# Later near sums and chunk ends in the second pass over the adjacency matrix, and the constants of the ranking as a scheduled step

## The chip, the cores and the metric

The kernel runs on one core of a Trainium2 chip. The metric is the device time of one execution in microseconds (us). The core has five engines with queues of their own that run beside each other and wait for each other by semaphores: TensorE (PE, matrix products), VectorE (DVE), ScalarE (ACT), GpSimd (POOL, here mostly the issuer of gathers) and SyncE (SP, the issuer of the large loads). Transfers run on 16 DMA engines.

## The reference

Four layers of a graph network follow each other on the same graph with N = 2708 nodes and 128 features. Each ends with a layer normalization of `x + layer(x)`. Cut to what matters here, the first two are:

```python
# layer 0
z  = leaky_relu(lap_mul(A, x) @ W1 + b1, 0.1)
S  = exp(-dist(z, z) / 2);  keep the 4 largest of each row, the rest 0
A2 = S + A
x  = layernorm(x + lap_mul(A2, x) @ W2 + b2)     # lap_mul(A, x) = d * (A @ (d * x)), d = rowsum(A) ** -0.5
# layer 1
XW = x @ W;  s_col = XW @ a[:128];  s_row = XW @ a[128:]
den = exp(leaky_relu(s_row[:, None] + s_col[None, :], 0.01))
num = A @ den
x  = layernorm(x + A @ ((den / num) @ XW))
```

All of it is in 32-bit floats. Layers 2 and 3 are products with the same `A`.

## The kernel before, in words

The 2708 rows are 22 tiles of 128 (the last has 20 rows); the columns are six chunks of 512, 512, 512, 512, 384 and 276, so that chunks 0 to 3 hold four tiles each and chunks 4 and 5 three each. The matrix is read as `adjT`. Six tiles of it stay in SBUF (`res`); the others come through a ring of four slots, filled by SP's loads (`load_panel`, L171 to L182).

The program has these stages: a first pass over the matrix (to about 165 us); the search for the four nearest nodes of each row (to about 300 us), where PE makes the distances, ACT copies them out and DVE finds the largest eight and their places (MAX8 and FIND_INDEX8, L649 and L650); the second pass, which multiplies by `A` again with the rows `y2` (295 to about 446 us); a ranking of the nodes, with a third pass (to about 530 us); and the second layer by blocks and the last layers.

The second pass is the place of the change. `by_panels` (L189) runs 132 products on PE: for each chunk, 16 tiles from the ring and five from `res`, and for the last tile's 20 rows three products at a time. A product of 512 columns is two passes on PE. After each product it calls `due.tick`. `Due` (L31 to L50) is a list of steps with a due number: `at(n, f)` puts step f at product n, and `tick` runs all steps that have come due, in the order of their numbers and, for equal numbers, of their entry. PE, DVE and ACT have a written order in this part (`manual_schedule`, L965): their instructions run in the order in which the steps issue them. An instruction of such a step can still stand between earlier instructions of the search, where the scheduler places it. POOL and SP have no written order.

The steps of a chunk c are these.

- `sum_near(t)` (L683), once for each tile t, at product `near_at[t]` (L915). It multiplies a row tile by the node's own weight (L686, DVE), has POOL gather three rows for each node from `y2_rows` in DRAM (`gather_near`, L675, issued at L677) and adds them with their weights (L690, DVE). The gathered rows have nine buffers.
- `end_pass2(c, acc)` (L922) is called when a chunk's products are done. It sets the product n at which the chunk ends: at least three products behind the near sum of its last tile, 16 behind the end of the chunk before, and not before the products are done.
- At n, `finish` (L927): `add_near` (L692, PE at L697) adds the near sums to the chunk's sum, and ACT copies it out to `hT` (L929).
- At n + 2, `norm0` (L734): PE multiplies by `w2` (L737), DVE adds and normalizes (L742, then L272 to L277; ACT takes a square root at L242).
- At n + 9, `turn` (L751, PE at L755, ACT's copy at L758); at n + 11, `find_c` (L806, PE at L809, ACT's copy at L810, DVE at L814).
- From n + 13, `compare` (L836, DVE), `times_w` (L819, PE at L822), `rank_rows` (ACT at L859) and `rank_columns` (PE at L864), some products apart for each tile, and `keep_xw` (L825), which stores rows to `xw_rows` from POOL's queue.

With the numbers before, the near sums stand at products 24, 28, 33, 37, 42, ... 120, and the chunks end at products 40, 59, 77, 96, 112 and 132.

Ahead of these steps, the constants of the ranking (L718 to L729) are written by DVE: a memset of `rk_f`, three additions for `fold`, and a memset and a copy for `sel`. They lie in the memory of `near`, which the search has written and which POOL still reads (L575 to L584, `others`) when it orders the neighbours.

Of the kernel before, what the change touches and what calls it, by code (L numbers as in the profile page):

```python
# [22 lines left out]
CH = 4  # L23
MAGIC = 1.5 * 2**23
OOB = 4095
# [5 lines left out]
class Due:  # L31
# [5 lines left out]
    def at(self, n, f, *args):  # L37
        self.work.append((n, len(self.work), f, args))
        self.work.sort(key=lambda w: w[:2])
# [13 lines left out]
def kernel(  # L53
# [16 lines left out]
    nc = tc.nc  # L70
    N, D = x.shape
    assert D == P
    T = (N + P - 1) // P
# [10 lines left out]
    NCH = NB // CH  # L84
# [51 lines left out]
    ident = const.tile([P, P], F32, tag="ident", name="ident")  # L136
# [227 lines left out]
    with tc.tile_pool(name="knn", bufs=1) as knn:  # L364
# [261 lines left out]
        with tc.tile_pool(name="keys", bufs=3) as keys:  # L626

            for n, t in enumerate([*range(4, S), *range(4), *range(S, T)]):
                p = pw[t]
# [89 lines left out]
    spare = near.rearrange("p t k -> p (t k)")  # L719
    few_n, rk_f, neg_r = (spare[:, n * T : (n + 1) * T] for n in range(3))  # L720
    fold, sel = spare[:, 3 * T : 3 * T + 2 * NCH], spare[:, 3 * T + 2 * NCH : 3 * T + 2 * NCH + 2 * NB]
    nc.vector.memset(rk_f, float(OOB))
    nc.vector.tensor_add(fold, ident[:, : 2 * NCH], ident[:, 32 : 32 + 2 * NCH])
    for g in (64, 96):
        nc.vector.tensor_add(fold, fold, ident[:, g : g + 2 * NCH])
    nc.vector.memset(sel, 0.0)
    nc.vector.tensor_copy(
        sel.rearrange("p (a v) -> p a v", v=2 * CH)[:, :, :2], fold.rearrange("p (a v) -> p a v", v=2)
    )  # L729
    nc.vector.memset(rows_d, 0.0)  # L730
    add_bias(b2_sb)
    rk = rk_pool.tile([P, T], F32, tag="rk", name="rk")
# [179 lines left out]

    due = Due()
    at = due.at
    near_at = [24 + (23 * t) // 5 for t in range(T)]  # L915
    for t in range(T):
        at(near_at[t], sum_near, t)

    ended = [-16]
    behind_last = []  # L920
# [794 lines left out]
```

## Time and profile before

| what | value |
| --- | --- |
| median of 6 runs | 1098.14 us (1093.43 to 1105.49) |
| profiled execution | 1095.9 us, span 1094.2 us |
| PE | 1003.5 us busy, 92% of the span |
| DVE | 641.3 us, 59% |
| ACT | 338.4 us, 31% |
| POOL | 262.8 us, 24% |
| granted clock of TensorE, mean | 0.969 |
| `add_near` of chunk 0 starts | 328.02 us |
| the last `add_near` starts | 444.63 us |

How to read it: times inside the profile are microseconds from the span's start. A line of the order of time gives the start, the duration, the engine, the line of the kernel, the operation, the tiles (out<-in) and their shapes, how many instructions were merged, and in brackets the idle time of that engine just before and what ended it. "issue" is a wait for which the profile shows no releaser; "remote" is one that ended with a signal whose sender the profile does not name. The ends of PE's products are modelled by the profile. The granted clock is 1 at full speed.

### The profile page before, as it was taken

To read this page: it belongs to the slowest core of one execution; us is meant where nothing else is said; L and a number is where in the kernel's file an instruction comes from. 1 tells how busy PE (TensorE), PEld (TensorE's weight loads), DVE (VectorE), ACT (ScalarE), POOL (GpSimd) and SP (SyncE) were. 2 spreads that over 40 slices of the span, in tenths; PEclk is the share of its full clock that TensorE was granted. 3 is DMA by queue.
4 is the path that set the end of the run, shared out by engine and by line. 5 is a ranking of instruction groups with operands and counts; after the bars stand their busy time and mean duration, and the time that the engine had idled before them with its cause. 6 is when DMAs were issued, how large, how long until landed. Compare 5 with 4: busy or idle time off the path is not lost.

```text
span 1094.2 us, 11460 instructions
## 1 busy us (share of the span) xinstructions
PE 1003.5 (92%) x3691; PEld 484.6 (44%) x3691; DVE 641.3 (59%) x1354; ACT 338.4 (31%) x617; POOL 262.8 (24%) x334
## 2 busy tenths in 40 slices
PE   0798999999997898798799999999999999999996
PEld 0345544444443455643233333334444644565444
DVE  5984448999943477773398999998112112132122
ACT  0000125555501144612466776665001100011000
POOL 4000000000465564006584444430112100000000
PEclk9989999999998999699899999999999999999998
DMA  9999330000184556497545545555675875574752
GB/s 341 362 323 281 108 124 1 0 1 1 49 277 133 162 179 190 151 343 257 134 130 160 147 126 161 143 153 181 220 241 150 278 224 187 171 234 160 240 160 75
DMA packets 109380, 190.31 MB, mean 174 GB/s; under 512 B 13666, under 2 KB 46706, under 8 KB 109310
## 3 DMA queue, kind: packets, MB, share of 16 engines
q1 hardware_dynamic: 91408, 151.79, 42.8%
q0 software_dynamic: 17728, 37.62, 12.4%
q8 instruction: 31, 0.51, 0.2%
q14 instruction: 39, 0.32, 0.1%
q10 hardware_dynamic: 174, 0.08, 0.0%
HBM read 214.37 MB, written 4.16 MB: 200 GB/s over the span
## 4 chain that ended last, share of the span: by engine, by line
PE 78%; DVE 7%; DMA 5%; issue 4%; ACT 2%; another core or an unknown queue 2%; POOL 1%; SPq 1%; POOLq 0%; DVEq 0%; ACTq 0%
PE acc L204 32%; PE num L1519 9%; PE hacc L1376 9%; PE acc L647 8%; PE acc L428 7%; DMA res<-in_adjT 3%; PE acc L637 2%; PE acc L1270 2%; PE mis L285 1%; DVE where L650 1%; DMA got<-y_rows,where 1%; DMA part<-in_adjT 1%; DVE near L649 1%; DVE both L483 1%
## 5 line engine op out<-in xcount | busy, mean ns | idle before, releaser
L1397 POOL DMA_INDIRECT ring<-in_adjT,slot_i x88 | 96.3, 1094 | 115.5 <-PE num L1519 87.2
L1519 PE MATMUL num<-ring,lw 128*64 128x512 f32 (+1 forms) x528 | 115.7, 560 | 3.0 <-DVE err L1361 1.6
L1376 PE MATMUL hacc<-inv,xws 128*128 128x512 f32 (+1 forms) x264 | 111.7, 559 | 0.6 <-issue 0.3
L647 PE MATMUL acc<-zT,z 128*128 128x512 f32 (+4 forms) x264 | 108.6, 558 | 0.0
L1351 ACT ACTIVATE inv<-num,plain 128x1024 f32<-128x1024 f32 x88 | 80.6, 915 | 60.9 <-PE num L1519 36.6
L253 POOL TENSOR_TENSOR rstd<-rstd,minus_half 128x4 f32<-128x4 f32 (+1 forms) x18 | 17.3, 960 | 313.4 <-DVE rstd L252 313.4
L648 ACT COPY key<-acc 128x512 f32<-128x512 f32 (+3 forms) x132 | 70.3, 535 | 59.8 <-issue 29.8
L234 ACT COPY gb<-acc 128x512 f32<-128x512 f32 (+2 forms) x18 | 9.6, 535 | 251.1 <-PE acc L204 251.1
L1361 DVE TENSOR_TENSOR err<-inv,num 128x1024 f32<-128x1024 f32 x88 | 74.4, 854 | 20.1 <-ACT inv L1354 17.7
L204 PE MATMUL acc<-ring,y 128*128 128x512 f32 (+2 forms) x192 | 81.3, 554 | 0.5 <-POOL sim L584 0.5
L1376 PEld LDWEIGHTS hacc<-inv,xws 128*128 128x128 f32 x264 | 46.5, 189 | 77.6 <-issue 47.9
L677 POOL DMA_INDIRECT got<-y_rows,where x66 | 69.7, 1057 | 39.7 <-DVE near_sum L690 16.9
L204 PE MATMUL acc<-ring,xs 128*128 128x512 f32 (+2 forms) x192 | 77.7, 548 | 0.0
L1368 DVE SCALAR_TENSOR_TENSOR inv<-gb,g_inv,inv 128x1024 f32<-128x1024 f32 x88 | 77.1, 914 | 0.1
L204 PE MATMUL acc<-ring,carry 128*128 128x512 f32 (+2 forms) x192 | 74.5, 542 | 0.0
L204 PE MATMUL acc<-ring,m_rows 128*128 128x512 f32 (+2 forms) x192 | 74.3, 542 | 0.0
L1365 DVE SCALAR_TENSOR_TENSOR inv<-err,inv 128x1024 f32<-128x1024 f32 x88 | 72.5, 862 | 0.1
L647 PEld LDWEIGHTS acc<-zT,z 128*128 128x128 f32 (+1 forms) x264 | 47.5, 188 | 54.9 <-issue 49.4
L1354 ACT ACTIVATE inv<-inv 128x1024 f32<-128x1024 f32 x88 | 67.6, 768 | 2.8
L649 DVE MAX8 near<-key 128x8 f32<-128x2708 f32 (+1 forms) x22 | 65.5, 2979 | 3.9 <-ACT key L648 3.9
L575 POOL TENSOR_TENSOR slot_e<-near,sim 128x44 f32<-128x44 f32 (+2 forms) x3 | 0.7, 244 | 273.9 <-DVE d2inv L603 267.2
L650 DVE FIND_INDEX8 where<-near,key 128x8 uint32<-128x2708 f32 (+1 forms) x22 | 65.4, 2973 | 0.0
(357 smaller groups left out, 1354.4 us busy)
## 6 DMA issues: line engine op xcount, KB each, us to landing
ring<-in_adjT SPq DMA_DIRECT2D x86, 1024.0 KB
ring<-in_adjT SPq DMA_DIRECT2D x19, 768.0 KB
part<-in_adjT SPq DMA_DIRECT2D x12, 1024.0 KB
ring<-in_adjT SPq DMA_DIRECT2D x19, 552.0 KB
res<-in_adjT SPq DMA_DIRECT2D x4, 1280.0 KB
more<-in_adjT SPq DMA_DIRECT2D x4, 1024.0 KB
part<-in_adjT SPq DMA_DIRECT2D x3, 768.0 KB
part<-in_adjT SPq DMA_DIRECT2D x3, 552.0 KB
```

What stands on the lines that cost most here:

```text
L204: nc.tensor.matmul(accs[c][: lhsT.shape[-1], :w], lhsT=lhsT, rhs=src, start=start, stop=stop)
L428: nc.tensor.matmul(accs[c][:, : cw[c]], lhsT=y[:, i, :], rhs=src[:, : cw[c]], start=first, stop=last)
L647: nc.tensor.matmul(pks[c][:p, : cw[c]], lhsT=z2[:, :p], rhs=zT[:, cs], start=False, stop=True)
L649: nc.vector.max(near[:p, t, :], key[:p])
L650: nc.vector.max_index(where[:p, t, :], near[:p, t, :], key[:p])
L1351: nc.scalar.activation(inv, num[:, :w], AF.Ln, scale=plain[:, 0:1], bias=plain[:, 1:2])
L1361: nc.vector.tensor_mul(err, inv, num[:, :w])
L1365: nc.vector.scalar_tensor_tensor(inv, err, 2.0, inv, op0=ALU.subtract, op1=ALU.mult)
L1368: nc.vector.scalar_tensor_tensor(inv, gb[:, col : col + w], g_inv[:, q : q + 1], inv, op0=ALU.max, op1=ALU.mult)
L1376: nc.tensor.matmul(haccs[:, o:e], lhsT=xws[:, q, :], rhs=inv[:, o:e], start=(q == 0), stop=(q == NQ - 1))
L1397: nc.gpsimd.indirect_dma_start(out=rows[i][:KC, n, :], out_offset=None, in_=adj_half[:, :], in_offset=bass.IndirectOffsetOnAxis(ap=slot_i[ ...
L1519: nc.tensor.matmul(num[n * (BJ + 2) : (n + 1) * (BJ + 2), o:e], lhsT=lw[:, 2 * q + n, :], rhs=rows[i][:, n, c0 + o : c0 + e], start=True, ...
```

## The change

Two things change. The near sums stand at products `31 + (17 * t) // 4`, that is 31, 35, 39, 43, 48, ... 120, a step of 4.25 products instead of 4.6; with the rules of `end_pass2` the chunks then end at products 46, 63, 80, 97, 113 and 132. And the six instructions for the ranking's constants become a function that is a step at product 27 (`near_at[0] - 4`).

```diff
@@ -719,14 +719,17 @@
     spare = near.rearrange("p t k -> p (t k)")
     few_n, rk_f, neg_r = (spare[:, n * T : (n + 1) * T] for n in range(3))
     fold, sel = spare[:, 3 * T : 3 * T + 2 * NCH], spare[:, 3 * T + 2 * NCH : 3 * T + 2 * NCH + 2 * NB]
-    nc.vector.memset(rk_f, float(OOB))
-    nc.vector.tensor_add(fold, ident[:, : 2 * NCH], ident[:, 32 : 32 + 2 * NCH])
-    for g in (64, 96):
-        nc.vector.tensor_add(fold, fold, ident[:, g : g + 2 * NCH])
-    nc.vector.memset(sel, 0.0)
-    nc.vector.tensor_copy(
-        sel.rearrange("p (a v) -> p a v", v=2 * CH)[:, :, :2], fold.rearrange("p (a v) -> p a v", v=2)
-    )
+
+    def set_constants():
+        nc.vector.memset(rk_f, float(OOB))
+        nc.vector.tensor_add(fold, ident[:, : 2 * NCH], ident[:, 32 : 32 + 2 * NCH])
+        for g in (64, 96):
+            nc.vector.tensor_add(fold, fold, ident[:, g : g + 2 * NCH])
+        nc.vector.memset(sel, 0.0)
+        nc.vector.tensor_copy(
+            sel.rearrange("p (a v) -> p a v", v=2 * CH)[:, :, :2], fold.rearrange("p (a v) -> p a v", v=2)
+        )
+
     nc.vector.memset(rows_d, 0.0)
@@ -912,9 +915,10 @@
     due = Due()
     at = due.at
-    near_at = [24 + (23 * t) // 5 for t in range(T)]
+    near_at = [31 + (17 * t) // 4 for t in range(T)]
     for t in range(T):
         at(near_at[t], sum_near, t)
+    at(near_at[0] - 4, set_constants)
```

## The prediction

> **What bounds the kernel now.** I read the chain of waits first: PE carries 78% of the chain that ended last, so a change pays only where it takes idle time or slow clock from PE. Then the waits of PE within the second pass (294 to 470 us), the largest of them:
>
> ```profile
> PE mis L737 <- issue: 5.4, 2, 4.7
> PE acc L697 <- issue: 4.4, 1, 4.4
> PE mis L755 <- DVE xs L277: 3.0, 1, 3.0
> PE mis L809 <- ACT xT L758: 2.6, 1, 2.6
> ```
>
> The columns are total us, times, longest. L697 is `add_near`, L737 `norm0`, L755 `turn`. All waits of PE up to the last `add_near` (444.63) come to 17.9 us; that is all the change can touch. Then the same stretch in order of time on each engine (start, us, engine, line, ..., idle time before it):
>
> ```profile
> 328.02 0.83 PE L697 MATMUL acc<-ident,near_sum 128*128 128x128 f32 x6
> 333.24 0.79 PE L697 MATMUL acc<-ident,near_sum 128*128 128x128 f32 x2 [4.38 <-issue]
> 333.82 3.62 PE L204 MATMUL acc<-res,y 128*128 128x512 f32 x4
> 338.20 2.08 PE L737 MATMUL mis<-w,hT 128*128 128x128 f32 x8 [0.76 <-issue]
> ...
> 343.97 3.60 PE L204 MATMUL acc<-ring,y 128*128 128x512 f32 x8
> 350.60 1.10 PE L755 MATMUL mis<-ident,xs 128*128 128x128 f32 x4 [3.04 <-DVE xs L277]
> ...
> 361.65 1.05 PE L697 MATMUL acc<-ident,near_sum 128*128 128x128 f32 x8
> ...
> 369.34 1.47 PE L737 MATMUL mis<-w,hT 128*128 128x128 f32 x8 [4.69 <-issue]
> ```
>
> ```profile
> 289.10 0.16 DVE L723 TENSOR_TENSOR near<-ident 128x22 f32<-128x22 f32 x1 [2.44 <-issue]
> ...
> 332.44 0.74 DVE L690 SCALAR_TENSOR_TENSOR near_sum<-got,sim,near_sum 128x128 f32<-128x128 f32 x2 [1.75 <-DMA got<-y_rows,where]
> ...
> 346.78 1.13 DVE L742 SCALAR_TENSOR_TENSOR xs<-mis,d2inv,xs 128x128 f32<-128x128 f32 x4 [9.51 <-remote]
> ```
>
> ```profile
> 337.56 0.59 ACT L929 COPY hT<-acc 128x512 f32<-128x512 f32 x1 [29.86 <-issue]
> ...
> 368.70 0.59 ACT L929 COPY hT<-acc 128x512 f32<-128x512 f32 x1 [6.12 <-remote]
> ```
>
> ```profile
> 342.86 1.00 POOL L677 DMA_INDIRECT got<-y_rows,where  x1 [0.30 <-issue]
> 352.17 1.00 POOL L677 DMA_INDIRECT got<-y_rows,where  x1 [8.31 <-DVE near_sum L690]
> ...
> 366.66 1.00 POOL L677 DMA_INDIRECT got<-y_rows,where  x1 [0.30 <-issue]
> ```
>
> Three things stand here. PE reaches the near sum of tile 3 at 328.85, but DVE has it at 333.18 (332.44 + 0.74). After that wait PE is slow: four passes of 512 columns take 3.62 us, 0.85 each, against 0.43 elsewhere; the window 320 to 340 shows a granted clock of 0.81. And three times PE's work reaches ACT or DVE late: `add_near` of chunk 0 ends at 334.03 and ACT copies at 337.56 (3.5 late); `norm0` ends at 340.28 and DVE starts at 346.78 (6.5 late); `add_near` of chunk 1 ends at 362.70 and ACT copies at 368.70 (6.0 late). Each waits for PE alone in the built program. Two of them end 1.0 and 2.9 us after POOL's unbroken runs of gathers (last ends 343.86 and 367.66). I do not know the cause; that the late ones go with these runs is an inference.
>
> **The change part by part.**
>
> Constants (six vector instructions). The edit says that they leave the search. The built order of the changed kernel says otherwise: the memset and the first addition still stand between the MAX8 of 283.70 and the FIND_INDEX8 after it, the two other additions and the last pair where they were. Their wait of 2.44 us (by its place for POOL, which ends its last read of `near` at 289.04) is on the chain and stays. Cost 0; bounds -2.4 (it does leave) and +0.2 (the last pair on a later gap). Only one 0.27 us multiply of near sum 0 moves, from 304.47, a gap in which DVE waits for ACT until 305.44, to after the constants, where DVE waits 6.67 us for its first gathered row: 0.
>
> Near sums 0 to 4. In the built order DVE runs them in one row before `norm0` of chunk 0, as now, and POOL's gathers before them keep their order. Gathers, not due times, pace them, so near sum 3 is still done at 333.18: 0, bounds 0 and +1.
>
> End of chunk 0, product 40 to 46. PE now runs six more products, five from `res` and one from `ring`, before `add_near`. 12 passes at 0.43 are 5.16 us, so it arrives at 328.02 + 5.16 = 333.18, just as the sum is ready. The 4.38 us wait is filled with work, and the slow passes after it go too. But nothing behind it comes sooner: `add_near` at 333.2, ACT's copy at 337.56, `norm0` at 338.20, DVE at 346.78, the first normalized tile at 350.56, `turn` at 350.60. PE reaches `norm0` at 334.1 + 1.7 = 335.8 and waits 2.4, then does `norm0` (1.05) and seven products (6.02), is at `turn` at 345.3 and waits 5.3 where it waited 3.04. At 350.60 it is six products further: -5.16.
>
> End of chunk 1, product 59 to 63. `norm0` of chunk 1 stands at product 65, not 61. Before it PE has ten products (8.6), `turn` (0.94), `find_c` (0.86), three `times_w` (0.66) and `add_near` (0.89), 11.95 in all: 362.5, some 363.7 with a slow window after the 5.3 us idle time. Near sum 7 now stands before the second comparison on DVE (about 357.7, was 358.3), so it is no wait. If ACT hears at 368.70 again, `norm0` is again at 369.34 and PE is four products ahead, 3.44, less one `times_w` that it still owes, 0.22: -3.2. What is queued behind the waiting `norm0` on PE is the rest of chunk 2. The bounds of this step: the signal at 360.95 was only 1.36 late; so prompt, `norm0` is at 363.7 + 1.36 + 0.6 for the copy = 365.6, another -3.7; or 6.0 late from the later `add_near`, 370.3, +1.0. I take 368.70, since the run of gathers that it goes with is set by DVE's near sums 5 to 8, which keep their places after `norm0`.
>
> Chunks 2 to 5 end at products 80, 97, 113, 132 (now 77, 96, 112, 132). Chunk 2 ends 15 products after `norm0` of chunk 1 instead of 16, so its chain comes 0.9 sooner, the later ones 2.5 to 3.2. Near sum 15 now ends 5.0 us after `find_c` of chunk 2 begins (401.20; the first comparison ends at 404.83 and a near sum takes 1.4), and PE has six narrow products, two `times_w` and the `find_c`, 5.3 us: no wait, with 0.3 to spare. At the end ACT is nearly full (14.2 of 20 us in 440 to 460) and its copy for chunk 5 waited only 0.54 us for PE; chunk 4's chain gains 0.46 less than PE, so up to +0.3. POOL, which now has twelve gathers and not nine between two stores of `xw_rows`, has its last gather out at 424.78 for a sum at 433.2: 0. SP's loads keep their order and follow PE's releases; no wait of PE in this pass names one: 0.
>
> Sum: 0 + 0 - 5.16 + 1.94 + 0.3 = -2.9 us. The profiled execution took 1095.9 us (span 1094.2); so 1093.0 in its terms. It lies 2.2 below the median of 1098.14, so I predict 1098.14 - 2.9 = 1095.2.
>
> A rule that speaks against the change: "TensorE: Matmul & The Clock Gate" of the Trainium skill, in its part on the warmup mystery, says that one idle window of about 3.4 us halves TensorE's clock until a busy window follows. The rows: 4.38 us idle before 333.24 gave slow passes until about 342.6, 4.1 us lost in all (3.62, 2.08 and 4.06 us for work that takes 1.88, 1.05 and 2.74 elsewhere); 4.69 before 369.34 lost 1.7; 3.04 before 350.60 lost nothing (four passes 1.88). So it agrees; half of one such window, 1.7 us, is the estimate by the page for the new 5.3 us at `turn`. By the rows it costs between 0 and 4.1. Either lies before the wait for chunk 1, which ends at 369.34 in both cases; so the sum stays, unless that wait goes.
>
> **The rivals.**
>
> Chunk 1's signal becomes prompt. If `add_near` ends before about 361 (no slow window), the 1.36 row applies instead of the 6.00: the 4.69 us wait goes, and with it the slow passes after 369.34 (1.7, as 1.47 us for `norm0` against 1.05 and the passes behind it). -2.9 - 4.7 - 1.7 = -9.3: 1088.8. For it: 360.95 and 362.70 lie only 1.75 apart, and my arrival falls between 359.5 and 363.7. Against: the run of gathers still lasts until 367.7.
>
> Slower: a third chunk falls into a late signal. Chunk 2's `add_near` was heard at once (388.97, copy 389.00). It now comes about a microsecond sooner, with PE ahead of POOL's third run of gathers. If its signal is 6.0 late, `norm0` waits about 6.0 and slow passes add 1.7: -2.9 + 7.7 = +4.8, 1102.9. It decides from 2.9 us of such lateness on. Against: that run has breaks (384.79 waited for DVE), and its signals were prompt.
>
> The gain is only moved. The signal stays 6.0 late after an `add_near` that slow passes push beyond 364; `norm0` is at 371 to 372 and PE's lead of four products is gone: 0, 1098.
>
> The constants do leave the search, against the built order: 2.4 more, 1092.8.
>
> **How the numbers follow.** My forecast 0.46, prompt signal 0.26, slower 0.12, moved 0.11, constants 0.05. Half a per cent, 5.5 us, is about what a measurement of this kernel can tell from no change. Faster by more than that (below 1092.6): the prompt case and a part of the two others below the median, 0.31. Slower (above 1103.6): the upper half of the slower rival and what I have not seen, 0.09. Same: 0.60. The likeliest case's own range is 1092 to 1098; the range to hold 8 in 10 reaches to the prompt case and most of the slower one, 1088 to 1102.
>
> **What would show it.** In the changed profile: `add_near` of chunk 0 without an idle time above 1 us before it, and the passes after it at 0.43; a wait of about 5 us at `turn` that ends near 350.6; a wait at `norm0` of chunk 1 that ends near 369; the 2.4 us gap between MAX8 and FIND_INDEX8 still there; the last `add_near` near 441.7. It is wrong if ACT's and DVE's starts behind `add_near` and `norm0` of chunk 0 come sooner than 337.6 and 346.8 (then late signals follow PE's idling, not POOL), or if chunk 2 or 3 gets a new wait.

## The result and the profile after

| | before | after |
| --- | --- | --- |
| median, us (runs) | 1098.69 (84) | 1104.13 (42) |
| ratio, 95% interval | | 1.0053 [1.0038, 1.0067] |
| profiled execution, us (span) | 1095.9 (1094.2) | 1100.0 (1098.2) |
| mean granted clock of TensorE in it | 0.969 | 0.962 |

The changed kernel is slower by 0.5%, some 5.8 us. The prediction had 1095.2, a range of 1088 to 1102, and 0.09 for slower: it was wrong by its sign.

PE's waits in the second pass of the changed kernel (total us, times, longest):

```profile
PE mis L740 <- ACT hT L933: 15.9, 3, 11.5
PE rk L867 <- DVE mask L844: 3.9, 3, 1.8
```

L740 is `norm0`. The wait at `add_near` has gone, as predicted, and so has the one at `turn`, which was to grow to 5.3 us. In their place `norm0` waits 15.9 us for ACT's copy of `hT`. The same in order of time, PE first, then ACT, DVE and POOL:

```profile
328.08 4.45 PE L204 MATMUL acc<-res,y 128*128 128x512 f32 x10
332.37 1.02 PE L204 MATMUL acc<-ring,y 128*128 128x512 f32 x2
333.23 1.05 PE L697 MATMUL acc<-ident,near_sum 128*128 128x128 f32 x8
334.12 1.88 PE L204 MATMUL acc<-ring,y 128*128 128x512 f32 x4
347.48 2.08 PE L740 MATMUL mis<-w,hT 128*128 128x128 f32 x8 [11.48 <-ACT hT L933]
349.35 8.06 PE L204 MATMUL acc<-ring,y 128*128 128x512 f32 x14
357.24 0.60 PE L758 MATMUL mis<-ident,xs 128*128 128x128 f32 x4
...
372.94 1.49 PE L740 MATMUL mis<-w,hT 128*128 128x128 f32 x8 [4.09 <-ACT hT L933]
```

```profile
346.84 0.58 ACT L933 COPY hT<-acc 128x512 f32<-128x512 f32 x1 [39.12 <-remote]
372.31 0.59 ACT L933 COPY hT<-acc 128x512 f32<-128x512 f32 x1 [6.84 <-remote]
```

```profile
349.60 1.13 DVE L745 SCALAR_TENSOR_TENSOR xs<-mis,d2inv,xs 128x128 f32<-128x128 f32 x4 [13.59 <-PE mis L740]
```

```profile
342.71 1.00 POOL L677 DMA_INDIRECT got<-y_rows,where  x1 [0.30 <-issue]
354.98 0.99 POOL L677 DMA_INDIRECT got<-y_rows,where  x1 [11.27 <-DVE near_sum L690]
```

`add_near` of chunk 0 starts at 333.23, on the predicted moment and without a wait. Its modelled end is 334.28, but ACT copies the sums only at 346.84, 12.6 us later (3.5 in the kernel before). POOL's last gather of the first run ends at 343.71; ACT follows 3.1 us behind it. In the kernel before, only the second hand-off of chunk 0 (PE's `norm0` to DVE) came out behind the run of gathers (346.78, run's end 343.86), because ACT had its copy done at 337.56, in the middle of the run. Now the first hand-off comes out behind it, and the second can only start then. I call a signal of PE "held" when it comes so late.

Two views of both kernels side by side, busy time by stage: the window's length, then PE, its weight loads, DVE, ACT and POOL with their instructions, then the granted clock, the DMA share and GB/s. Before:

```profile
312.00:446.00 134.00, 116.09 (x527) 65.47 (x525) 71.46 (x268) 36.62 (x78) 73.65 (x71) 0.94 0.59 182
```

After:

```profile
312.00:446.00 134.00, 114.23 (x521) 65.61 (x520) 71.62 (x268) 36.26 (x76) 74.09 (x70) 0.91 0.57 182
```

From the first gather to the end of the pass the clock falls from 0.94 to 0.91. That is 4 us of full speed in 134 us; how much of it falls into PE's waits, where it costs nothing, these lines don't tell. The lines of the stages are of one profile each.

### The profile page after: what moved, and what is told of

It is laid out like the page before. It is cut to its first block, busy times and chain, and to the rows that moved or that the text cites. A ratio compares the mean times of both kernels' runs of the same rounds, so it can differ in the third digit from the quotient of the medians.

```text
span 1098.2 us, 11461 instructions
## 1 busy us (share of the span) xinstructions
PE 1004.8 (91%) x3691; PEld 486.6 (44%) x3691; DVE 641.6 (58%) x1354; ACT 338.3 (31%) x617; POOL 264.4 (24%) x334
## 4 chain that ended last, share of the span: by engine, by line
PE 77%; DVE 7%; another core or an unknown queue 5%; DMA 4%; ACT 3%; issue 3%; POOL 1%; SPq 0%; ACTq 0%; POOLq 0%; DVEq 0%
PE acc L204 31%; PE num L1523 9%; PE hacc L1380 9%; PE acc L647 8%; PE acc L428 8%; PE acc L637 2%; DMA res<-in_adjT 2%; PE acc L1274 2%; PE mis L285 1%; DVE where L650 1%; DMA part<-in_adjT 1%; ACT junk L862 1%; DVE near L649 1%; DVE both L483 1%
```

## The experiments

Each ratio is against the kernel before on the same chip, with its 95% interval. The runs behind the first result came in five sets of five rounds each. "Run's end" is the end of the last gather of POOL's first unbroken run, "ACT" the start of the copy of chunk 0's sums, "late" the time between the two, all in the one profile of that kernel. In `wait46_b` the run has one break, of 0.94 us at 338.74, before its end at 344.57.

| set (before, us) | kernel | ratio | run's end | ACT | late |
| --- | --- | --- | --- | --- | --- |
| first result | after | 1.0053 [1.0038, 1.0067] | 343.71 | 346.84 | 3.1 |
| 1 (1097.06) | gate_after | 1.0024 [0.9991, 1.0057] | 330.68 | 333.04 | |
| 1 | c0_only | 1.0041 [1.0017, 1.0065] | 345.60 | 348.94 | 3.3 |
| 1 | c1_only | 0.9980 [0.9958, 1.0002] | 344.02 | 333.08 | |
| 1 | const_out | 0.9974 [0.9943, 1.0004] | 339.62 | 342.46 | 2.8 |
| 2 (1096.30) | got6 | 0.9987 [0.9964, 1.0011] | 338.87 | 341.33 | 2.5 |
| 2 | got3 | 1.0039 [1.0018, 1.0059] | broken up | 335.87 | |
| 2 | gate0_69 | 1.0064 [1.0037, 1.0090] | 330.27 | 332.50 | |
| 2 | c0_56 | 1.0020 [1.0000, 1.0041] | 345.05 | 348.12 | 3.1 |
| 3 (1065.41) | wait46 | 1.0010 [0.9987, 1.0033] | 343.50 | 339.03 | |
| 3 | got6_before | 1.0003 [0.9977, 1.0029] | 338.39 | 332.19 | |
| 3 | got6_const | 0.9989 [0.9963, 1.0016] | 335.11 | 332.98 | |
| 3 | got5 | 1.0017 [0.9996, 1.0039] | broken up | 332.74 | |
| 4 (1095.23) | after_b | 1.0038 [1.0003, 1.0073] | 345.69 | 348.31 | 2.6 |
| 4 | wait46_b | 1.0038 [1.0012, 1.0064] | 344.57 | 346.48 | 1.9 |
| 4 | got6_before_b | 0.9946 [0.9909, 0.9984] | 339.25 | 335.45 | |
| 4 | got6_const_b | 0.9967 [0.9944, 0.9990] | 335.81 | 338.48 | 2.7 |
| 5 (1099.79) | split0 | 1.0074 [1.0047, 1.0102] | 344.20 | 347.22 | 3.0 |
| 5 | split_all | 0.9957 [0.9928, 0.9985] | 335.96 | 338.71 | 2.8 |

### Which part of the change loses

One part at a time, on the kernel before. `c0_only` and `c1_only` write the chunks' ends out by hand:

```diff
-        n = max(due.n + 1, near_at[chunk_tiles[c][-1]] + 3, ended[-1] + 16)
+        n = [46, 59, 77, 96, 112, 132][c]        # c0_only; c1_only: [40, 63, 77, 96, 112, 132]
```

> The kernel before with chunk 0's end at product 46 instead of 40 and nothing else changed (chunk 1's end stays at 59). If chunk 0's move alone brings the loss: ACT's copy goes from 337.56 to about 346.8, DVE behind norm0 from 346.78 to about 349.6, PE waits 10 to 12 us at norm0; as chunk 1's add_near now stands 13 products behind chunk 0's and not 17, its signal wait is longer too: 3 to 9 us slower than before. If the loss came from chunk 1's later end or from the later chunks: 0 to 5 us faster, as the prediction had it for this part (-5.2).

> The kernel before with chunk 1's end at product 63 instead of 59 and nothing else changed. If chunk 0's move alone brings the loss: chunk 0 as before (337.56, 346.78, 350.60), norm0 of chunk 1 at 369 to 372 with PE four products further: 1 to 4 us faster than before. If chunk 1's later end brings it: about 5 us slower.

In `c0_only`, PE first, then ACT:

```profile
331.16 1.05 PE L697 MATMUL acc<-ident,near_sum 128*128 128x128 f32 x8
...
349.58 2.08 PE L737 MATMUL mis<-w,hT 128*128 128x128 f32 x8 [15.65 <-ACT hT L929]
```

```profile
348.94 0.58 ACT L929 COPY hT<-acc 128x512 f32<-128x512 f32 x1 [43.31 <-remote]
```

Chunk 0's later end alone gives 1.0041, 4.5 us slower, with ACT's copy at 348.94 and a wait of 15.65 us at `norm0`; the longer wait at chunk 1 did not come (`norm0` of chunk 1 at 366.93, without a wait). Chunk 1's later end alone gives 0.9980, 2.2 us faster with an interval that just takes in no change; its profile does not show the gain, since `norm0` of chunk 1 stands at 375.15 behind a wait of 4.34 us (369 to 372 was expected) and the last `add_near` at 444.82 (444.63 before). So the loss comes with chunk 0's end. The two parts together would be +2.3; what the later chunks add was not run alone, and the intervals of some 2.5 us to each side leave room for it.

`const_out` puts the constants where they do leave the search: a step at product 27 in the kernel before, whose first near sum stands at 24 and so comes ahead of them on DVE.

```diff
+    def set_constants():
         nc.vector.memset(rk_f, float(OOB))
...
     near_at = [24 + (23 * t) // 5 for t in range(T)]
...
+    at(27, set_constants)
```

> The kernel before with the constants of the ranking written at product 27, after near sum 0 at 24, and nothing else changed; in this order they do leave the search on DVE (behind near sum 0's three gathered rows). If the 2.44 us gap ahead of the first addition is on the path of the search, all behind it comes that much sooner: 2.4 us faster. If it is hidden (DVE waits 6.7 us for its first gathered row anyway): 0.

0.9974, 2.9 us faster with an interval from 6.3 faster to 0.4 slower: near the 2.4 of the gap, and not settled against 0. Its one profile is of an execution of 1102.39 us, 6.7 above the median of its runs (1095.71), so what it shows need not hold for the others. It has the first gather at 308.23 (312.54 before), near sum 3 ready before PE arrives, no idle time ahead of `add_near` (327.25), and ACT's copy at 342.46, 2.8 behind the run's end, with a wait of 13.08 us at `norm0`. Chunk 0 ends at product 40 here, as in the kernel before. So it is not the later product by itself that leaves the signal in the run.

### Is it POOL's gathers

`gate_after` is the changed kernel with POOL stopped around the two hand-offs of chunks 0 and 1. The row indices of later gathers are copied, behind a small copy that reads the statistics DVE writes after `norm0` (the gathers of these tiles then read their indices from the copy, in lines not shown here):

```diff
+    def open_gate(t0, c):
+        t1 = min([t for t in gates if t > t0] + [T])
+        nc.gpsimd.tensor_copy(where_g[:, t0, :2], mv[:, chunk_tiles[c][0], :])
+        nc.gpsimd.tensor_copy(where_g[:, t0:t1, :], where[:, t0:t1, TOPK : TOPK + 3])
```

> The changed kernel, but POOL may issue the gathers of tiles 5 to 8 only after DVE has the first statistics behind norm0 of chunk 0, and those of tiles 9 on only after the same of chunk 1; nothing on PE, DVE, ACT and SP changes its place. Theory A (a signal of PE to ACT or DVE that falls due while POOL issues gathers back to back is held until that run is through): the first run ends near 332 instead of 343.7, ACT copies chunk 0 at 334.3 to 335.5 (346.84 in the changed kernel), DVE starts behind norm0 near 337.5 (349.60), the 11.48 us wait at norm0 falls below 3, the slow passes behind it go, chunk 1's 4.09 goes too: 10 to 17 us faster than the changed kernel, 5 to 12 faster than the kernel before. Theory B (PE itself reports late when it runs without a break; POOL has no part in it): ACT still copies chunk 0 about 12 us after add_near, and the time is that of the changed kernel or worse, since near sums 5 to 7 come later.

Its order of time on PE, ACT, POOL and DVE:

```profile
331.95 1.05 PE L708 MATMUL acc<-ident,near_sum 128*128 128x128 f32 x8
...
334.56 1.05 PE L751 MATMUL mis<-w,hT 128*128 128x128 f32 x8
335.45 6.17 PE L204 MATMUL acc<-ring,y 128*128 128x512 f32 x14
341.46 0.60 PE L769 MATMUL mis<-ident,xs 128*128 128x128 f32 x4
...
355.97 0.80 PE L708 MATMUL acc<-ident,near_sum 128*128 128x128 f32 x2 [5.07 <-DVE near_sum L701]
```

```profile
333.04 0.58 ACT L946 COPY hT<-acc 128x512 f32<-128x512 f32 x1 [26.59 <-PE acc L708]
```

```profile
329.68 0.99 POOL L680 DMA_INDIRECT got<-y_rows,where  x1 [0.30 <-issue]
337.26 0.19 POOL L688 CAST where<-mv 128x2 uint32<-128x2 f32 x1 [6.58 <-DVE mv L273]
```

```profile
334.66 0.35 DVE L701 SCALAR_TENSOR_TENSOR near_sum<-got,sim,near_sum 128x128 f32<-128x128 f32 x1 [0.33 <-DMA got<-y_rows,where]
```

Nothing but POOL's work and its waits differs from the changed kernel, and ACT copies at 333.04, with `add_near`'s modelled end at 333.00. PE does not wait at all up to `turn`, which runs at 341.46 instead of 357.24, and its fourteen passes take 6.17 us and not 8.06. So POOL's gathers hold the signal, and PE's report is not late by itself. In this profile gathered rows were still on their way when ACT copied (DVE waits for the last of them until 334.66), so the hold seems to go with the issuing and not with the transfers; no run separates the two on purpose. The time, though, is 1.0024 and not 5 to 12 us faster: the 7 us in which POOL stood still are missing later. `add_near` of chunk 1 waits 5.07 for near sum 7, and the runs of gathers from 364.70 on have few breaks; ACT's copy for `find_c` at 423.60 waits 3.81 for a held signal. The last `add_near` is at 446.9 (444.86 in the changed kernel).

`got6` and `got3` leave the order of PE, DVE and ACT alone and change how far POOL may run ahead of DVE:

```diff
-    got_pool = late.enter_context(tc.tile_pool(name="got", bufs=9, side="right"))
+    got_pool = late.enter_context(tc.tile_pool(name="got", bufs=6, side="right"))    # got3: bufs=3
```

> The changed kernel with 6 buffers for gathered rows instead of 9; the order of work is the same on every engine but for one store of xw_rows on POOL. POOL can then run only 6 gathers ahead of DVE, and its first unbroken run has 21 gathers, not 24. Theory A (the signal is held until the run is through and comes about 3 us behind it): the run ends 3.9 us sooner, near 339.8, ACT copies chunk 0 near 342.9 (346.84 in the changed kernel), DVE starts behind norm0 near 345.7 (349.60), PE's wait at norm0 is 7.6 instead of 11.48: 2 to 5 us faster than the changed kernel, so -1 to +3 against the kernel before. Theory B (the lateness is PE's own): ACT at 346.8 within 1 us, and the time of the changed kernel.

> The changed kernel with 3 buffers for gathered rows instead of 9, the order of work on PE, DVE and ACT unchanged. POOL can run only 3 gathers ahead of DVE and has to stop for it again and again. Theory A: a hold lasts no longer than the next stop, so ACT copies chunk 0 within 5 us of add_near's end, and the hand-offs of the later chunks are prompt too; the price is that a near sum can no longer be fetched ahead, so add_near waits for DVE by up to 5 us at chunks 1 to 5. Between -8 and +5 against the changed kernel, by which of the two is larger. Theory B: ACT about 12 us after add_near, and the price on top: +3 to +10 against the changed kernel.

ACT's copy in `got6`, and the gather behind the first run, whose idle time gives the run's end (349.47 - 10.60 = 338.87):

```profile
341.33 0.59 ACT L933 COPY hT<-acc 128x512 f32<-128x512 f32 x1 [34.63 <-remote]
```

```profile
349.47 0.99 POOL L677 DMA_INDIRECT got<-y_rows,where  x1 [10.60 <-DVE near_sum L690]
```

Three gathers fewer, and the copy comes with the run's end: the end 4.8 us sooner, the copy 5.5, `norm0`'s wait 7.02. The time falls from 1.0053 to 0.9987, some 7 us, where 2 to 5 were expected; by the 1.0038 that the changed kernel has in a later set it is 5.6, and the intervals do not tell these apart. With three buffers the hand-offs are prompt (ACT at 335.87, `add_near`'s modelled end 335.83), and the price is as feared: four waits of `add_near` for DVE, 11.3 us in all. 1.0039 is within what was expected (-8 to +5 against the changed kernel).

### Can PE work through the hold, or the hold be moved

`c0_56` gives PE ten more products ahead of `add_near`; `gate0_69` is `gate_after` with the stop at chunk 0 alone and the later chunks' ends moved.

```diff
+        n = [56, 71, 85, 100, 115, 132][c]        # c0_56
+    near_at = [31 + (17 * t) // 4 if t < 5 else 39 + 4 * t for t in range(T)]
...
+        n = [46, 69, 84, 99, 115, 132][c]         # gate0_69
+        if c in (0,):
+            gates[min(t for t in range(T) if near_at[t] > n + 2)] = c
```

> The changed kernel with chunk 0's end ten products later still (56), the near sums from tile 5 on at products 59, 63, 67, ... so that they stay behind norm0 of chunk 0 on DVE, and the other ends at 71, 85, 100, 115 and 132. Theory A: the run of gathers is the same 24, so ACT copies chunk 0 near 347 whenever add_near ran; PE has ten products more (8.6 us) to do in that time, arrives at add_near near 342 and waits 2 to 4 us at norm0 instead of 11.48, with at most one slow window: 4 to 8 us faster than the changed kernel. If what counts is the number of products ahead of add_near (each later end makes PE's report later): ACT near 354 and a wait of 10 us or more: the time of the changed kernel or slower.

> The changed kernel with the stop of POOL at chunk 0 alone (gathers of tiles 5 on wait for the first statistics behind norm0 of chunk 0), and with the ends of the chunks at products 46, 69, 84, 99, 115 and 132, so that chunk 1's add_near comes after near sum 7 has its rows. Expected: chunk 0 as with both stops (ACT at 333, DVE at 335.7, turn at 341.5), no wait of 5 us at chunk 1's add_near, PE there some ten products ahead of the changed kernel; from chunk 2 on POOL has to make up 7.6 us, so its runs are longer and signals of the later chunks are held in them. If the gain of chunk 0 survives to the end of the pass: 4 to 8 us faster than the kernel before. If the later runs of gathers take it back: 0 to +3 against before.

`c0_56` moves `add_near` to 343.17, 10 us later, and ACT copies at 348.12, 3.1 behind the run's end at 345.05. PE waits 2.81 and not 11.48: as the theory has it, the moment is the run's and not `add_near`'s. The time is 1.0020, 3.6 us below the changed kernel's ratio, a little less than the 4 to 8 expected. `gate0_69` has chunk 0 prompt (332.50), but the gathers put off make a second run of 21 that ends at 364.86, three more follow up to 369.91, and chunk 1's hand-off falls into it: ACT at 371.74 for an `add_near` of 356.68, 12.79 us of wait at `norm0`. 1.0064: the hold was only moved. Neither expectation had it that bad.

### What let the first signal through before

In the kernel before PE stood idle ahead of `add_near`. `wait46` gives the changed kernel that idle time back, with sixteen multiplies by one on DVE ahead of the last addition to near sum 3. Beside it stand three others: `got6_before` and `got5` (the kernel before with `bufs=6`, the changed one with `bufs=5`) and `got6_const` (the changed one with `bufs=6` and `at(near_at[0] + 2, set_constants)`).

```diff
             gather_near(got, t, TOPK + k)
+            for _ in range(16 if (t, k) == (3, TOPK - 2) else 0):
+                nc.vector.tensor_scalar_mul(g, g, 1.0)
```

> The changed kernel with sixteen multiplies by one (about 0.28 us each, 4.5 in all) on DVE ahead of the last addition to near sum 3, so that PE, at product 46, waits about 4 us for it as it does in the kernel before at product 40; POOL's run of 24 gathers keeps its pace. Theory A2 (PE's idle time ahead of add_near lets its signal through the run of gathers, and the changed kernel lost that): ACT copies chunk 0 within 5 us of add_near, at 338 to 342 (346.84 in the changed kernel), only the second hand-off waits for the end of the run (DVE near 346.8), turn is free near 350.6: faster than the changed kernel by 3 to 7 us, although 4 us of waiting were added. Theory A1 (a signal is held to the end of the run whatever PE did before it; that one got through in the kernel before has another reason): ACT near 346.8, and the time of the changed kernel or up to 2 us more.

> The kernel before with 6 buffers for gathered rows instead of 9, nothing else changed but the place of one group of gathers behind a store of xw_rows on POOL. The first run of gathers ends 3.9 us sooner. Theory A: the hand-off that is held to its end in the kernel before (norm0 to DVE, 346.78) comes at 342.5 to 343.5, turn near 346.7: 0 to 4 us faster than before. If it is as fast as the changed kernel with 6 buffers or faster, the later ends bring nothing by themselves even with the shorter run; if it is slower by 2 us or more, the later ends do pay once the run is out of their way.

> The changed kernel with 6 buffers and with the constants written at product 33, behind near sum 0, where they do leave the search. The two effects measured alone add if they are independent: 6 buffers -7 and constants -2 to -3 against the changed kernel, so 1 to 5 us faster than the kernel before. If the run of gathers, which then starts some 3 us sooner, only meets add_near at another point, nothing is added: 0 to 1 against the changed kernel with 6 buffers.

> The changed kernel with 5 buffers for gathered rows. The run of gathers is 20 long and ends 1.3 us before that with 6 buffers: ACT copies chunk 0 near 340 (341.33 with 6), 1 us faster than with 6 if nothing else waits. With 3 buffers add_near waited 11.3 us for near sums; if 5 are already too few, its waits for DVE grow above 2 us and the time is 1 to 3 us above that with 6.

These four give no answer. Beside them the kernel before took 1065.41 us, and in none of the four profiles was a signal of PE held in the second pass: `got6_const` copies at 332.98 with `add_near`'s modelled end at 332.94 and POOL gathering up to 335.11. All four ratios lie within 0.2% of before. Three of the four were run once more, in another set, beside the changed kernel itself:

> The changed kernel itself once more, beside the next three. In the last four runs, on a chip on which the kernel before takes 1065 us, no signal of PE was late: ACT and DVE heard within 1.1 us in the middle of a run of gathers. So the hold belongs to some chips only. If this chip holds signals (the kernel before near 1097): ACT copies chunk 0 near 346.8, 3 us behind the run's last gather, and the time is 3 to 8 us above that of before. If it does not (before near 1065): ACT copies within 1.1 us of add_near near 334, the 4.38 us wait is gone and nothing takes its place, and the time is 1 to 5 us below that of before, as the prediction had it.

> The changed kernel with the sixteen multiplies ahead of the last addition to near sum 3 again. On a chip that holds signals: theory A2 (idle time of PE ahead of add_near lets its signal through): ACT at 338 to 342, turn free near 350.6, 3 to 7 us faster than the changed kernel; theory A1 (held to the run's end whatever PE did before): ACT near 346.8, 0 to 2 us above the changed kernel. On a chip that does not: 0 to 4 us above the changed kernel, for the wait alone.

> The kernel before with 6 buffers again. On a chip that holds signals: DVE behind norm0 of chunk 0 at 342.5 to 343.5 instead of 346.8, 0 to 4 us faster than before. On a chip that does not: within 1 us of before, as in the last runs.

> The changed kernel with 6 buffers and the constants at product 33 again. On a chip that holds signals: 6 buffers alone gave the time of before (-7 against the changed kernel), so with the constants -1 to -5 against before if the two add. On a chip that does not: -1 to -3 against before, as in the last runs.

Here signals were held again. The changed kernel is at 1.0038, ACT at 348.31, 2.6 behind the run's end: the first result repeats. `wait46_b` on PE and ACT:

```profile
333.25 0.83 PE L699 MATMUL acc<-ident,near_sum 128*128 128x128 f32 x6
339.47 0.79 PE L699 MATMUL acc<-ident,near_sum 128*128 128x128 f32 x2 [5.39 <-DVE near_sum L692]
347.12 2.07 PE L742 MATMUL mis<-w,hT 128*128 128x128 f32 x8 [3.74 <-ACT hT L935]
```

```profile
346.48 0.58 ACT L935 COPY hT<-acc 128x512 f32<-128x512 f32 x1 [38.74 <-remote]
```

PE idles 5.39 us ahead of the last near sum, more than the 4.38 of the kernel before, and ACT still hears 1.9 behind the run's end. So idle time alone does not let the signal through (theory A2 falls). The added work, 5.0 us on DVE, cost nothing that shows: 1.0038, as the changed kernel, with intervals of some 3 to 4 us to each side.

The last idea was that signals leave one by one during a run and that `add_near` now sends four in a row. `split0` adds three of chunk 0's near sums at product 40, as the kernel before does, and the fourth at 46; `split_all` does so in each chunk, on top of `got6_const`.

```diff
...
+        early = ts[:-1] if c == 0 else []        # split_all: in every chunk
+        at(n - 6, add_near, c, acc, early)
...
         def finish():
-            add_near(c, acc)
+            add_near(c, acc, ts[len(early) :])
```

> The changed kernel, but of chunk 0's four near sums PE adds three at product 40, where the kernel before adds them, and only the fourth at product 46; no other instruction on PE, DVE, ACT or POOL changes its place. Theory A3 (while POOL gathers back to back, PE's signals still get out, but one by one, some 3 us apart; add_near sends four in a row, so the last, for which ACT waits, is behind the others): three of the four leave at 328 and drain by about 337, and ACT copies chunk 0 at 336 to 341 as in the kernel before, in the middle of the run; only norm0's signal to DVE waits for the run's end (about 346.8), turn is free near 350.6: 2 to 6 us faster than the changed kernel. Theory A1 (every signal waits for the end of the run): ACT near 346.8 and the time of the changed kernel. On a chip that holds no signals: the time of the changed kernel.

> The changed kernel with 6 buffers, the constants at product 33, and in every chunk all near sums but the last added six products ahead of the chunk's end. Beside the same kernel without the split (0.9967 of before, 1091.0 us where before took 1095.2), theory A3 gives another 1 to 4 us, as chunk 0's and chunk 1's signals get out before the run's end: 4 to 8 us faster than before. Theory A1: the ratio of the kernel without the split, 0.995 to 0.999.

```profile
328.45 0.83 PE L697 MATMUL acc<-ident,near_sum 128*128 128x128 f32 x6
334.27 0.41 PE L697 MATMUL acc<-ident,near_sum 128*128 128x128 f32 x2
347.86 2.08 PE L740 MATMUL mis<-w,hT 128*128 128x128 f32 x8 [11.46 <-ACT hT L936]
```

In `split0` ACT copies at 347.22, 3.0 behind the run's end (344.20), and the ratio is 1.0074; in `split_all` the copy is 2.8 behind its run's end: theory A3 falls too. The signal got through in mid-run in three profiles (before 337.56, `c1_only` 333.08, `got6_before_b` 335.45). In all three chunk 0 ends at product 40, three near sums are added ahead of the fourth, and PE idles 3.25 to 4.38 us between. Early additions and idle time together do not explain it either: `wait46_b` has both, at product 46 (near sums at 333.25 and 339.47), and its signal was held. The trace's records of PE's semaphore don't settle it. They give the moments at which its count moved (some may be missing):

```
before     ... 324.76  331.10  333.95  346.76        run of gathers 312.54 to 343.86
after      ... 324.82  328.26  346.65 (five at once)                312.56 to 343.71
after_b    ... 326.52  329.96  337.01  344.04  346.84  348.25       314.39 to 345.69
wait46_b   ... 328.27  333.07  337.30  339.43  342.96  346.45       312.63 to 344.57
wait46     ... 327.91  332.20  333.06  333.28  333.51  333.73  339.01   nothing held
```

During a run single moves get out, some 2 to 7 us apart, or none does: none for 18 us in the first profile of the changed kernel, two in `after_b`, which is the same kernel. PE's idling does not decide it: in that first profile PE stood idle from 336.00 on, and nothing moved before 346.65. What decides it stays open.

### A version that beats both

Where signals are held, three kernels with six buffers beat both kernels: the kernel before with 6 buffers at 0.9946 [0.9909, 0.9984], the changed kernel with 6 buffers and the constants at product 33 at 0.9967 [0.9944, 0.9990], the same with all near sums split at 0.9957 [0.9928, 0.9985]. The changed kernel with 6 buffers alone (`got6`) is not told from before. In the first of these DVE starts behind `norm0` at 341.82, 2.6 behind its run's end at 339.25, where it started at 346.78. These 5.0 us fit the 5.9 that the kernel gained (0 to 4 were expected). As the kernel before with 6 buffers is no slower than the changed one with 6, the later ends show no gain of their own even with the shorter run. In the set in which nothing was held, six buffers made no difference (1.0003).

## Why the prediction was wrong

- The constants: right. The wait ahead of their first addition is still there (289.14, 2.41 us), so they stayed in the search. `const_out` puts the price of their leaving at 2.9 us, near the 2.4 given as the bound and not clear of 0.
- Near sums 0 to 4: right. Near sum 3 was ready when PE came at 333.23 (333.18 predicted).
- The end of chunk 0: this step failed. The arrival and the filled wait were right. "But nothing behind it comes sooner: ... ACT's copy at 337.56" was also meant to say that nothing comes later. It took the moment of one hand-off from the profile of before and kept it, while the step changed the very thing around it. It was 346.84, and 348.94, 348.31 and 347.22 in three more profiles with the same end (`c0_only`, `after_b`, `split0`). `turn` came at 357.24 and not 350.60. Six products further on at 0.86 would be 355.76 at the old pace, so the step was worth +1.5 and not -5.16.
- "and the slow passes after it go too": wrong as well. The 11.48 us of idle time brought them back: fourteen passes take 8.06 us where `gate_after` needs 6.17, and `norm0` 2.08 where it needs 1.05, 2.9 us in all. The rule of the Trainium skill that was weighed ("TensorE: Matmul & The Clock Gate", the warmup mystery: an idle window of about 3.4 us halves the clock until a busy window follows) agrees with these rows.
- The end of chunk 1: wrong in its moment too. `norm0` was to stay at 369.34 with PE four products further. Run alone (`c1_only`, with chunk 0 prompt) it stood at 375.15: the run of gathers went on to 371.95, and ACT copied at 374.52. The 2.2 us that this kernel gained lie near the 3.2 of the forecast, with an interval that contains both that and zero; since the profile does not have the mechanism, the agreement is luck or noise. In the changed kernel its premise was gone: the run of gathers was taken to keep its place, but near sum 5 waits on DVE behind `norm0` of chunk 0, so POOL went on at 354.98 (352.17 before) and that run ended at 370.83 (367.66). `norm0` of chunk 1 came at 372.94, outside the bounds given (365.6 to 370.3).
- Chunks 2 to 5: no new wait at chunk 2 or 3, as predicted. The last `add_near` was at 444.86; before it was at 444.63, and 441.7 was predicted.
- The slower rival had the right mechanism, a late signal of 6 us and more, at the wrong place: at chunk 2, and not at chunk 0's own first hand-off, for which the page had a late start in plain sight. What it named as the sign of an error was a start sooner than 337.6 and 346.8; it came later.

So the hold explains why the gain did not come in this pair of profiles. By the prediction's own way of counting, chunk 0's end is worth +1.5, and `norm0` of chunk 1 came at 372.94 where the old pace would have it at 369.34 + 3.22 = 372.56; the last `add_near` is 0.2 us later, and 2.9 sooner was predicted.

Not settled is where the medians lose their 4 to 6 us. In the one pair of profiles the pass ends 0.2 us later and the block phase starts 4.2 later (537.25 for 533.03). But in `after_b` the last `add_near` is at 447.15, 2.5 later than before, and the stretch between it and the block phase takes 88.2 us, as in the kernel before (88.4), and not the 92.4 of the first profile. Single profiles scatter here by as much as is sought. What all runs have is the mean granted clock: 0.9615 over the 42 runs of the changed kernel, 0.9644 to 0.9663 for the kernel before in the four sets in which signals were held. Span times what is missing to 1 is 42.5 us against 36.9 to 39.0, so 3.5 to 5.6 us more of it; `c0_only` has 41.7 beside 36.9, `got6` 38.8 beside 39.0. `gate_after` (41.6 beside 36.9, for a ratio of 1.0024) and `c0_56` (37.9 beside 39.0, for 1.0020) follow this less well. The clock records of the traces say much the same: between 300 and 545 us the clock stands at one half for 44.4 us in the kernel before, for 58.0 and 54.6 in the two profiles of the changed kernel and for 58.0 in `c0_only`, but for 51.2 in `c1_only`, which lost nothing. That fits a loss by longer idle times and the slow clock behind them, but it is a correlation and no proof.

## What to carry to other kernels

When a hand-off in the profile starts later than its producer's modelled end, find what it is late with before an edit is priced on its moment; a late moment is not a fixed time that the schedule can be built around. Here the measure was another engine's unbroken run of gathers, so the cheap remedy was a shorter run (six buffers for nine), not another order of PE's work. An idle time that is filled upstream is gained only if the next hand-off was not waiting for something else anyway.

## What the runs showed of the hardware that I had not expected

- A signal of PE to ACT or DVE can stay out up to 16.7 us (`c0_only`: `add_near`'s modelled end 332.21, ACT 348.94) while POOL issues gathers back to back, 1.0 us each with 0.3 between. It comes 1.9 to 3.3 us behind the last of them: ten profiles with ACT's copy, with run's ends from 335.81 to 345.69. The Trainium skill ("Perfetto Trace Analysis", Tensor Engine Instruction) says that a matmul's end in the profile is estimated and that the semaphore update follows PSUM's acknowledgement and has to propagate; it gives no time for that. With POOL still, ACT starts 0.04 us behind the modelled end (`gate_after`).
- It isn't so in every set of runs. The same kernel, with its first gather at 312.27 and 312.63, reached the block phase at 507.8 in set 3 and at 532.8 in set 4. The first line is `wait46` (set 3), the second `wait46_b` (set 4):

```profile
312.00:508.00 196.00, 179.64 (x1078) 100.33 (x1078) 122.99 (x404) 61.81 (x135) 100.34 (x96) 0.92 0.70 227
```

```profile
312.00:508.00 196.00, 173.29 (x975) 97.38 (x975) 118.00 (x394) 54.56 (x113) 88.04 (x87) 0.90 0.65 212
```

  From there to the span's end (1068.2 and 1094.0) it is 560 and 561 us; the 25 us lie ahead of it, in the stretch that has the gathers. Sets 3 and 5 carry the same chip number, and only one of them held signals, so I can't put it down to a chip. The changed kernel itself was not run in a set without the hold; whether it gains its 3 us there is open.
- Added work need not show: 5.0 us of multiplies on the path to `add_near` (`wait46_b`) left the ratio at that of the changed kernel, 1.0038 both, with intervals of some 3 to 4 us to each side.
